# Order of the six products of a convolution set, and where their sums and ends are kept, in a two-layer Trainium2 kernel

## The chip, the cores and the metric

The kernel runs on one core of one Trainium2 chip, as one program. The metric is device time in microseconds (us) of one execution. Five engines work side by side and meet through semaphores: TensorE (PE in the profile; its weight loads are PEld), VectorE (DVE), ScalarE (ACT), GpSimd (POOL), and SyncE (SP), which here issues most DMAs. Each engine takes its own instructions strictly in the order in which the program lists them. PE writes only into PSUM, an accumulator memory of 8 banks of 512 float32 per partition; DVE and ACT read PSUM and carry results on to SBUF, the working memory.

## The reference, cut to what matters

Layer 0 (group norm, a four-direction state-space scan, a projection) and layer 1 act on x of shape 4 x 96 x 128 x 128. The change touches layer 1 alone. For each image x there is a split x1 = relu part, x2 = the rest, both normed, and then

```python
key   = unfold(conv2d(x1, aw1))          # 3x3, 96 -> 96 channels
qry   = unfold(conv2d(x2, aw2))
attn  = softmax(einsum('bckl,bqkl->bqck', key, qry).reshape(B, C, C*9) / sqrt(C*9))
value = conv2d(x1, aw3)
y1    = layer_norm(conv2d(value, attn.reshape(C, C, 3, 3)))   # weights made from the data
y2    = layer_norm(conv2d(x2, w_conv2)) * x1
out   = xr + conv2d(concat([y1, y2]), w_full) + b_full
```

So an image needs five 3x3 convolutions: aw1 and aw3 on x1, aw2 and w_conv2 on x2, and last the attention's own weights on value. All of it is float32.

## The kernel before, in words

**Stages.** From 0 to about 3685 us of the profiled execution come layer 0 for all four images and the convolutions of image 0, which are done directly, tap by tap (the group at L2156). From 3685 to about 6440 us comes the attention part of layer 1 (`attention`, L1946), and only there do the functions that the change touches run. After that the last image is written out.

**A convolution by products.** In the attention part a 3x3 convolution is done along the width with six products for every four neighbouring output columns: six planes of differences of the input (0 to 5, made earlier) are each multiplied with their own transformed weights on PE, which gives P0 to P5, and the outputs of the four columns are, with AA = 2,

- out 0 = P0 + (P1 + P2) + (P3 + P4)
- out 1 = (P1 - P2) + AA (P3 - P4)
- out 2 = (P1 + P2) + AA^2 (P3 + P4)
- out 3 = (P1 - P2) + AA^3 (P3 - P4) + P5

P1 to P4 are called the inner products here, P0 and P5 the outer ones (the code's `ends`). One call of `products` (L1443) is one set: 12 rows (`AR`) of an image, six products. Each product is two matmuls of 128 input rows (`main`, L1464, on the tiles `ya` and `yb`) and then small ones of 32 rows each (`rest`, L1479), because 3 taps x 96 channels are 288 = 128 + 128 + 32 rows. A float32 matmul is recorded as two matmuls in the profile.

**Which sets run.** Image 0 has 11 sets, one for each strip of 12 rows, with the attention's weights (`wa`; 96 output channels, 384 columns). Images 1 to 3 have those 11, and before them, in each strip, two maps of two sets: one of 128 output channels and 384 columns, whose output goes to `ring` and `own`, and one that puts two half strips side by side, 2 x 64 output channels and 192 columns, whose output goes to `own` or `oc` (weights `wd`). That is 44 + 132 = 176 sets. Between the sets of images 1 to 3, `taps.some` puts transposes of the ring (`both`, L1757) whose results ACT copies to `kt` (L1762), and the products of key and query (`multiplied`, L1632), which DVE adds to `sm` (L1645).

**PSUM tiles.** Sets, transposes and key-query products all take tiles called `two` from one pool (`pairs_of`, L1439): two banks each, three of them. A set takes three tiles: before, one for P0 and P5, which I call the outer tile; one for P1 and P3, the odd tile; one for P2 and P4, the even tile. PE may write into a tile only when every reader of the tile's last user is done. The other two banks of PSUM hold `bank` tiles of the work beside.

**A set before the change.** `products` does P0 and P5 first (the list `TWO`), and `outer` has ACT copy them to SBUF (`ends`, L1537), which frees the outer tile. Then come P1, P3, P2, P4 (`FOUR`). `sums` has ACT copy the odd tile to SBUF (`odd`, L1537), which frees it. Then DVE works on `odd` and the even tile: four operations on half tiles make P3 - P4 and P3 + P4 in SBUF (`wide`, L1551, L1552) and P1 - P2 and P1 + P2 in place in PSUM (L1553, L1554). Then it writes out 1 and out 2 (L1559), adds `ends` in place (L1557), and writes out 0 and out 3 (L1559). The even tile is free only after the last of these. Each of the four outputs takes one input from SBUF (`wide`) and one from PSUM.

**Who sets the order.** `later` is a list of postponed work that runs one step at each `tick()`. The program text gives each instruction a priority. From the attention part on, a scheduler of the tile framework places the instructions on their engines and picks a PSUM tile for each `two`, by priority and by its own model of when things are ready. The order on every engine is fixed by that before the run. Beside the sets runs other work (`light`): the norm of layer 0's output of the next image (L960, L1009), its split into x1 and x2 (L1250, L1254, and the difference planes on POOL and DVE: `pl`, `plv`, L1393 to L1429), and the output of the image before (L2271 to L2325). `co_run` (L298) interleaves the two by costs that the generators yield.

**Feeding.** `Attention.load` (L1885) brings the planes of a strip as three pairs of planes, by the list `PAIRS`; `turn` (L1913) has ACT copy parts of them to `yb` (L1925), six copies a strip, in the same order of pairs. `weights` (L1670) makes the attention's weights at the end of an image's maps: it runs a few steps of the last set before the softmax and a few behind it, to give PE work beside it.

Of the kernel before, what the change touches and what calls it, by code (L numbers as in the profile page):

```python
# [9 lines left out]
F32 = mybir.dt.float32  # L10
# [22 lines left out]
TN = W // TW  # L33
# [38 lines left out]
def kernel(  # L72
# [1272 lines left out]

    PAIRS = ((0, 5), (1, 3), (2, 4))
    PAIR = {i: k for k, pair in enumerate(PAIRS) for i in pair}
    SLOT = {i: pair.index(i) for pair in PAIRS for i in pair}  # L1350
    FOUR = ((1, 0), (3, 32), (2, 64), (4, 96))
# [87 lines left out]
    def pairs_of(ps):  # L1439

        return ps.tile([128, 2, CH], F32, name="two", tag="two")

    def products(ps, jobs, ws, later, evac, threes=False, fill=()):  # L1443


        w1, w2, w3 = ws
        share = sum(r * (e - p) for p, e, _, _, _, r in jobs) / (128.0 * AR)

        def tiles(v, o, r):
            v = v[:, o * TN : (o + r) * TN]  # L1450
            if threes:
                return v.rearrange("p (i q t) -> p q i t", q=3, t=TN)
            return v

        def of(to, r):
            to = to[:, : r * TN]
            if threes:
                return to.rearrange("p (q i t) -> p q i t", q=3, t=TN)
            return to

        def main(to, i):
            for k, w in enumerate((w1, w2)):
                for p, e, c, t, o, r in jobs:
                    nc.tensor.matmul(  # L1464
                        of(to[p:e], r),
                        lhsT=w[:, i, c : c + e - p],
                        rhs=tiles(t[k][PAIR[i]][:, SLOT[i]], o, r),
                        start=(k == 0),
                        stop=False,
                    )  # L1470

        def rest(j, group, to):
            for i, q in group:
                for p, e, c, (ya, _, (yc,)), o, r in jobs:
                    if q < 64:
                        rhs = tiles(yc[q : q + 32], o, r)
                    else:
                        rhs = tiles(ya[PAIR[i]][q : q + 32, SLOT[i]], o + (2 if q == 64 else 1), r)
                    nc.tensor.matmul(  # L1479
                        of(to[i][p:e], r),  # L1480
                        lhsT=w3[q : q + 32, j, c : c + e - p],
                        rhs=rhs,
                        start=False,
                        stop=True,
                    )

        outer, sums = evac
        fill = iter(fill)

        def beside():  # L1490
            for f in (next(fill, None),):
                if f:
                    f()

        a = pairs_of(ps)
        to = {0: a[:, 0], 5: a[:, 1]}
        for i, _ in TWO:
            main(to[i], i)
            beside()
            later.tick()  # L1500
            yield 1.3 * share
        rest(1, TWO, to)
        outer(a)
        later.tick()
        yield 0.4 + 0.4 * share
        a, b = pairs_of(ps), pairs_of(ps)
        to = {1: a[:, 0], 3: a[:, 1], 2: b[:, 0], 4: b[:, 1]}
        for i, _ in FOUR:
            main(to[i], i)
            beside()  # L1510
            later.tick()
            yield 1.3 * share
        rest(0, FOUR, to)
        sums(a, b)
        later.tick()
        yield 0.4 + 0.6 * share

    def outputs(pool, m, n, parts, later, then):

        got = []

        def at(v, k):
            if isinstance(v, list):
                return v[k]
            if len(v.shape) == 4:
                return v[:, :, k]
            return v.rearrange("p h (t k) -> p h t k", k=TW)[:, :, :, k]  # L1530

        def rows(v):
            return v.rearrange("p (h t) -> p h t", t=TN)

        def copy_of(x, name, bufs):
            t = pool.tile([128, 2, AR * TN], F32, name=name, bufs=bufs)[:m, :, :n]
            nc.scalar.copy(t, x[:m, :, :n])  # L1537
            return t

        def outer(c):  # L1540
            later(lambda: got.append(copy_of(c, "ends", 2)))

        def sums(a, b):
            def first():
                t = copy_of(a, "odd", 1)
                later(lambda: combined(t))

            def combined(t):
                w = pool.tile([128, 2, AR * TN], F32, name="wide", bufs=1)[:m, :, :n]
                ends, v = got[0], b[:m, :, :n]  # L1550
                nc.vector.tensor_sub(w[:, 1], t[:, 1], v[:, 1])  # L1551
                nc.vector.tensor_add(w[:, 0], t[:, 1], v[:, 1])  # L1552
                nc.vector.tensor_sub(v[:, 1], t[:, 0], v[:, 0])  # L1553
                nc.vector.tensor_add(v[:, 0], t[:, 0], v[:, 0])  # L1554
                for k, j, f in ((1, 1, AA), (2, 0, AA * AA), (0, 0, 1.0), (3, 1, AA**3)):
                    if k == 0:
                        nc.vector.tensor_add(v, ends, v)  # L1557
                    for p, e, o in parts:
                        nc.vector.scalar_tensor_tensor(  # L1559
                            at(o, k), rows(w[p:e, j]), f, rows(v[p:e, j]), ALU.mult, ALU.add  # L1560
                        )
                later(then)

            later(first)

        return outer, sums

    def by_threes(v, r):

# [9 lines left out]
    class Taps:  # L1579
# [4 lines left out]
        def __init__(self, ps, later, pool, slots, taps):  # L1584
            self.ps, self.later, self.pool, self.slots = ps, later, pool, slots
            self.taps = [(k, min(k + taps, KK)) for k in range(0, KK, taps)]
            self.sm = pool.tile([C, KK, C], F32, name="sm")
            self.rings = [pool.tile([128, 3, slots, PW], F32, name=f"ring{i}") for i in range(2)]
            for t in self.rings:
                nc.gpsimd.memset(t[:, :, :, 0:1].rearrange("p r i w -> p (r i) w"), 0.0)  # L1590
            self.groups, self.todo, self.rest = 0, [], ()

        def flat(self, m):
            return self.rings[m].rearrange("p r i w -> p (r i w)")
# [75 lines left out]
        def weights(self):  # L1670


            rest = iter(self.rest)
            self.later.flush()
            for _ in range(3):
                yield next(rest, 0.0)
            self.later.flush()
            while self.todo:
                yield from self.some(1)
                self.later.flush()  # L1680
            flat = self.sm.rearrange("p t o -> p (t o)")
            sc = 1.0 / math.sqrt(C * KK)
            mx = col("mx")
            nc.vector.reduce_max(mx, flat, AX.X)
            nc.vector.tensor_scalar(mx, mx, -sc, None, ALU.mult)
            den = col("den")
            nc.scalar.activation(flat, flat, AF.Exp, scale=sc, bias=mx, accum_out=den)
            nc.vector.reciprocal(den, den)
            nc.vector.tensor_scalar(flat, flat, den, None, ALU.mult)
            yield 4.0  # L1690
            for _ in range(2):
                yield next(rest, 0.0)

            v = self.flat(1)[0:C, : KK * C].rearrange("p (h w o) -> p h w o", h=3, w=3)
            for h in range(3):
                pT = self.part(C, 3 * C)
                for w in range(3):
                    nc.tensor.transpose(pT[:, w * C : (w + 1) * C], self.sm[:, 3 * h + w], ident)
                nc.vector.tensor_copy(v[:, h].rearrange("p w o -> p (w o)"), pT)
            wt = self.flat(0)[0:C, : 3 * NP * C].rearrange("p (h i o) -> p h i o", h=3, i=NP)  # L1700
            s = self.flat(1)[0:C, KK * C : 12 * C].rearrange("p (h o) -> p h o", h=3)
            products_weights(wt, v, s)
            self.wt = wt
            yield from rest
            self.later.flush()
            yield 4.0

    class PairTaps(Taps):
# [3 lines left out]
        def __init__(self, ps, later, pool):  # L1712
            self.ps, self.later, self.pool = ps, later, pool
            self.taps = [(0, 5), (5, KK)]
            sm = pool.tile([128, KK, C], F32, name="sm")
            self.sm = sm[0:C]
            self.spare = sm[96:128].rearrange("p t o -> p (t o)")
            self.rings = [
                pool.tile([128, 2, AR, JW], F32, name=f"ring{i}", tag=f"ring{i}") for i in range(2)
            ]  # L1720
            for t in self.rings:
                for j in range(TW):
                    nc.gpsimd.memset(t[:, :, :, JB * j + TN : min(JB * (j + 1), JW)], 0.0)
            self.todo, self.rest = [], ()

        def flat(self, m):
            return self.rings[m].rearrange("p s r w -> p (s r w)")
# [956 lines left out]
```

## Time and profile before

| what | value |
|---|---|
| median of 3 timed runs | 6458.6 us (6457.25 to 6462.66) |
| profiled execution, its own time | 6482.78 us |
| its span, first to last instruction | 6481.0 us |
| granted TensorE clock, mean | 0.887 |
| stretch 0 to 3685 us: busy PE, DVE, ACT, POOL | 2988, 2727, 2322, 2302 us |
| stretch 3685 to 6440 us (attention part) | shown below in the prediction |
| stretch 6440 to 6481 us: busy PE, DVE | 30.6, 19.5 us |

How to read the lines below. A row of groups has the line in the program, the engine, the operation, out<-in by the program's names, a shape and a count; behind the first bar the busy time in us and the mean of one in ns; behind the second bar the engine's idle time just before them and what ended most of it. A row of waits names an engine and the line that waited, what it waited for, the total in us, how often, and the longest. A row of the timeline has the start in us, the length in us, the engine, the line and, in square brackets, the idle time before it and what ended it. A row that begins with a stretch has its length and then, for each engine, busy us and the number of instructions, and last the granted clock, the share of DMA time, and GB/s.

### The profile page before, as it was taken

To read this page: it belongs to the slowest core of one execution; us is meant where nothing else is said; L and a number is where in the kernel's file an instruction comes from. 1 tells how busy PE (TensorE), PEld (TensorE's weight loads), DVE (VectorE), ACT (ScalarE), POOL (GpSimd) and SP (SyncE) were. 2 spreads that over 40 slices of the span, in tenths; PEclk is the share of its full clock that TensorE was granted. 3 is DMA by queue.
4 is the path that set the end of the run, shared out by engine and by line. 5 is a ranking of instruction groups with operands and counts; after the bars stand their busy time and mean duration, and the time that the engine had idled before them with its cause. 6 is when DMAs were issued, how large, how long until landed. Compare 5 with 4: busy or idle time off the path is not lost. (4 is left out here: it accounts for less than half of the span.)

```text
span 6481.0 us, 76143 instructions
## 1 busy us (share of the span) xinstructions
PE 5325.5 (82%) x23264; PEld 2306.2 (36%) x23264; DVE 4757.0 (73%) x7132; ACT 3792.2 (59%) x4770; POOL 3279.9 (51%) x2514
## 2 busy tenths in 40 slices
PE   6889988987887754989988588877888877889888
PEld 2333323322222111444433234345333445345543
DVE  4247878988999768988844785468874687988766
ACT  1247767777787676777632565366634665545542
POOL 1226757978889455969822344346313265023310
PEclk9899989988998666999998798888988888999989
DMA  6767777776775766675676775655776656966668
GB/s 154 175 156 193 197 206 191 216 211 165 205 196 157 214 179 213 196 208 176 192 189 182 189 217 158 165 157 153 215 195 171 174 141 165 245 173 179 184 168 217
DMA packets 884520, 1205.17 MB, mean 186 GB/s; under 512 B 220084, under 2 KB 736570, under 8 KB 871632
## 3 DMA queue, kind: packets, MB, share of 16 engines
q1 hardware_dynamic: 860496, 1145.35, 65.1%
q0 software_dynamic: 16208, 38.42, 2.3%
q10 hardware_dynamic: 7408, 16.53, 0.8%
q8 instruction: 187, 3.06, 0.2%
q14 instruction: 221, 1.81, 0.1%
HBM read 777.82 MB, written 345.62 MB: 173 GB/s over the span
## 5 line engine op out<-in xcount | busy, mean ns | idle before, releaser
L629 PE MATMUL bank<-y,wp 128*128 128x512 f32 (+3 forms) x3584 | 1315.6, 624 | 85.4 <-DMA y<-y 42.2
L862 POOL TENSOR_TENSOR y<-y,dl 128x1024 f32<-128x1024 f32 x384 | 1055.6, 2749 | 262.5 <-DVE dl L854 236.5
L829 POOL TENSOR_TENSOR dl<-dl,u 128x1024 f32<-128x1024 f32 x384 | 1008.2, 2626 | 264.7 <-ACT dA L805 123.5
L850 DVE TENSOR_TENSOR_SCAN dA<-dA,pBC 128x512 f32<-128x512 f32 x768 | 981.6, 1278 | 30.7
L1464 PE MATMUL two<-ya,wd 128*64 128x192 f32 (+3 forms) x2376 | 588.8, 422 | 197.8 <-ACT odd L1537 80.0
L629 PEld LDWEIGHTS bank<-y,wp 128*128 128x128 f32 (+3 forms) x3584 | 458.6, 169 | 755.4 <-issue 654.4
L743 PE MATMUL pBC<-xr,wbc 60*128 60x512 bf16 (+1 forms) x1536 | 460.7, 406 | 316.5 <-DVE dA L850 245.8
L2156 PE MATMUL bank<-y,wn 128*64 128x384 f32 (+5 forms) x2408 | 674.9, 505 | 54.7 <-DMA y<-x1d 31.6
L854 DVE TENSOR_TENSOR dl<-dA,pBC 128x512 f32<-128x512 f32 x768 | 528.3, 688 | 260.7 <-PE pBC L743 187.2
L1925 ACT COPY yb<-ya 64x768 f32<-64x768 f32 (+1 forms) x660 | 537.5, 814 | 196.1 <-PE two L1464 130.2
L672 ACT ACTIVATE dl<-pd,dtb 128x512 f32<-128x512 f32 x768 | 486.4, 684 | 190.0 <-PE pd L743 172.3
L1464 PE MATMUL two<-yb,wd 128*64 128x192 f32 (+3 forms) x2376 | 563.5, 407 | 4.0 <-ACT yb L1925 4.0
L833 DVE TENSOR_TENSOR pBC<-dl,pBC 128x512 f32<-128x512 f32 x768 | 527.5, 687 | 8.5 <-POOL dl L829 7.5
L2156 PEld LDWEIGHTS bank<-y,wn 128*64 128x64 f32 (+3 forms) x2408 | 309.8, 168 | 347.0 <-issue 164.1
L805 ACT ACTIVATE dA<-dl,negA 128x1024 f32<-128x1024 f32 x384 | 420.3, 1142 | 2.3
L1464 PEld LDWEIGHTS two<-ya,wd 128*64 128x64 f32 (+1 forms) x2376 | 265.9, 169 | 398.5 <-ACT odd L1537 90.6
L743 PEld LDWEIGHTS <-wbc 60*128 60x128 bf16 (+1 forms) x1536 | 103.7, 96 | 764.3 <-issue 750.7
L672 ACT ACT_TABLE_LOAD x248 | 318.2, 1283 | 93.8 <-PE pd L743 80.7
L1464 PEld LDWEIGHTS two<-yb,wd 128*64 128x64 f32 (+1 forms) x2376 | 293.7, 171 | 147.3 <-issue 34.1
L2265 POOL MEMSET o<- 1x1024 f32 x60 | 56.4, 947 | 540.6 <-PE bank L2320 220.4
L1009 PE MATMUL bank<-y,outws 96*96 96x512 f32 x512 | 312.1, 748 | 13.2 <-DVE r L1022 7.7
L1464 PE MATMUL two<-ya,wa 128*96 128x384 f32 (+1 forms) x528 | 231.1, 521 | 71.8 <-DMA wa<-watd 27.0
(316 smaller groups left out, 9370.8 us busy)
## 6 DMA issues: line engine op xcount, KB each, us to landing
u<-zb SPq DMA_DIRECT2D x192, 1024.0 KB
yms<-y SPq DMA_DIRECT2D x96, 512.0 KB
y<-yms SPq DMA_DIRECT2D x64, 768.0 KB
xn<-xnew SPq DMA_DIRECT2D x128, 384.0 KB
ya<-vp SPq DMA_DIRECT2D x120, 336.0 KB
y<-y SPq DMA_DIRECT2D x128, 258.2 KB
zb<-z SPq DMA_DIRECT2D x64, 512.0 KB
ya<-x1p SPq DMA_DIRECT2D x90, 336.0 KB
```

The lines of the kernel that those rows point to most:

```text
L629: nc.tensor.matmul(blocks(pz[p:e]), lhsT=ws[k][:, d, c : c + e - p], rhs=window(ys[k], at, d, n), start=(i == 0), stop=(i == len(terms) - 1),)
L672: nc.scalar.activation(dst, src, AF.Softplus, bias=bias)
L743: nc.tensor.matmul(p, lhsT=w[rows], rhs=xr[rows, at : at + CH], start=True, stop=True)
L805: nc.scalar.activation(live[m]["dA"], live[m]["dl"], AF.Exp, scale=negA[:, g % 3, k : k + 1])
L829: nc.gpsimd.tensor_mul(t, t, u_view(n))
L833: nc.vector.tensor_mul(p, live[n]["dl"][:, bass.ts(half, CH)], p)
L850: nc.vector.tensor_tensor_scan(h, h, p, init, ALU.mult, ALU.add)
L854: nc.vector.tensor_mul(live[n]["dl"][:, sl], live[n]["dA"][:, sl], live[n]["C", half])
L862: nc.gpsimd.tensor_add(v, v, t.rearrange("p (a b) -> p a b", b=W))
L1464: nc.tensor.matmul(of(to[p:e], r), lhsT=w[:, i, c : c + e - p], rhs=tiles(t[k][PAIR[i]][:, SLOT[i]], o, r), start=(k == 0), stop=False,)
L1925: nc.scalar.copy(yb[k][64 * h - 64 : 64 * h, :, :n], ya[k][0:64, :, h * TN : h * TN + n])
L2156: nc.tensor.matmul(pc[p:e, :n].rearrange("p (h w) -> p h w", w=W), lhsT=w[:, c : c + e - p], rhs=v[:, :, 0:W], start=(i == 0), stop=(i == ...
```

## The change

The inner products go first and the outer ones last. The list of pairs is turned in the same way, so planes 1 and 3 are loaded and copied first, then 2 and 4, then 0 and 5. ACT still copies the odd tile to SBUF. DVE then makes all sums and differences in two operations on whole tiles instead of four on half tiles, into one SBUF tile `sums` (128 x 2 x 2 x 384, one buffer; `wide`, 128 x 2 x 384, one buffer, and `ends`, 128 x 2 x 384, two buffers, go). Out 1 and out 2 are written from `sums` alone, both inputs in SBUF. The outer tile isn't copied by ACT any more: once P0 and P5 are there, DVE adds the first half of `sums` to it in place in PSUM, and writes out 3 and out 0 from it and `sums`. The even tile is free after the two operations; the outer tile is free after out 0. In `weights` the number of steps of the last set ahead of the softmax is 2 and behind it 3 for images 1 to 3 (before: 3 and 2), and stays 3 and 2 for image 0.

```diff
-    PAIRS = ((0, 5), (1, 3), (2, 4))
+    PAIRS = ((1, 3), (2, 4), (0, 5))
...
     def products(ps, jobs, ws, later, evac, threes=False, fill=()):
...
-        outer, sums = evac
+        sums, ends = evac
...
+        a = pairs_of(ps)
+        to = {1: a[:, 0], 3: a[:, 1]}
+        for i, _ in FOUR:
+            if i == 2:
+                b = pairs_of(ps)
+                to |= {2: b[:, 0], 4: b[:, 1]}
+            main(to[i], i)
+            beside()
+            later.tick()
+            yield 1.3 * share
+        rest(0, FOUR, to)
+        sums(a, b)
+        later.tick()
+        yield 0.4 + 0.6 * share
         a = pairs_of(ps)
         to = {0: a[:, 0], 5: a[:, 1]}
         for i, _ in TWO:
...
         rest(1, TWO, to)
-        outer(a)
+        ends(a)
         later.tick()
         yield 0.4 + 0.4 * share
-        a, b = pairs_of(ps), pairs_of(ps)
-        to = {1: a[:, 0], 3: a[:, 1], 2: b[:, 0], 4: b[:, 1]}
-        for i, _ in FOUR:
-            main(to[i], i)
...
-        rest(0, FOUR, to)
-        sums(a, b)
-        later.tick()
-        yield 0.4 + 0.6 * share
...
     def outputs(pool, m, n, parts, later, then):
-        got = []
+        made = []
...
-        def outer(c):
-            later(lambda: got.append(copy_of(c, "ends", 2)))
+        def out(k, x, f, y):
+            for p, e, o in parts:
+                nc.vector.scalar_tensor_tensor(
+                    at(o, k), rows(x[p:e]), f, rows(y[p:e]), ALU.mult, ALU.add
+                )
...
             def combined(t):
-                w = pool.tile([128, 2, AR * TN], F32, name="wide", bufs=1)[:m, :, :n]
-                ends, v = got[0], b[:m, :, :n]
-                nc.vector.tensor_sub(w[:, 1], t[:, 1], v[:, 1])
-                nc.vector.tensor_add(w[:, 0], t[:, 1], v[:, 1])
-                nc.vector.tensor_sub(v[:, 1], t[:, 0], v[:, 0])
-                nc.vector.tensor_add(v[:, 0], t[:, 0], v[:, 0])
-                for k, j, f in ((1, 1, AA), (2, 0, AA * AA), (0, 0, 1.0), (3, 1, AA**3)):
-                    if k == 0:
-                        nc.vector.tensor_add(v, ends, v)
-                    for p, e, o in parts:
-                        nc.vector.scalar_tensor_tensor(
-                            at(o, k), rows(w[p:e, j]), f, rows(v[p:e, j]), ALU.mult, ALU.add
-                        )
-                later(then)
+                u = pool.tile([128, 2, 2, AR * TN], F32, name="sums", bufs=1)[:m, :, :, :n]
+                v = b[:m, :, :n]
+                nc.vector.tensor_sub(u[:, :, 1], t, v)
+                nc.vector.tensor_add(u[:, :, 0], t, v)
+                out(1, u[:, 1, 1], AA, u[:, 0, 1])
+                out(2, u[:, 1, 0], AA * AA, u[:, 0, 0])
+                made.append(u)
+
+            later(first)
+
+        def ends(c):
+            def closed():
+                if not made:
+                    later(closed)
+                    return
+                u, v = made[0], c[:m, :, :n]
+                nc.vector.tensor_add(v, u[:, 0], v)
+                out(3, u[:, 1, 1], AA**3, v[:, 1])
+                out(0, u[:, 1, 0], 1.0, v[:, 0])
+                later(then)
...
     class Taps:
+            self.held = (3, 2)
...
     class PairTaps(Taps):
+            self.held = (2, 3)
```

## The prediction

> **What bounds the kernel now.** The change acts only in the attention part, so I read that stretch alone. The chain of waits at the end is no guide: it reaches back to 6421 us only. First the engines over the stretch:
>
> ```profile
> 3685.00:6440.00 2755.00, 2306.70 (x12304) 1199.11 (x12305) 2010.92 (x3490) 1470.59 (x1945) 972.57 (x1352) 0.89 0.68 181
> ```
>
> PE is busy 2307 of 2755 us (84%), DVE 73%, ACT 53%, POOL 35%. PE is the backbone and loses some 450 us. Next, what PE waited for in the stretch:
>
> ```profile
> PE two L1464 <- ACT odd L1537: 95.4, 37, 10.0
> PE two L1464 <- ACT kt L1762: 51.4, 30, 7.9
> PE two L1464 <- ACT ends L1537: 37.5, 18, 6.5
> ...
> PE two L1464 <- ACT yb L1925: 21.8, 15, 3.6
> ...
> PE two L1464 <- DVE sm L1645: 19.2, 19, 3.4
> PE two L1632 <- ACT odd L1537: 16.7, 16, 3.3
> ...
> PE two L1632 <- DVE ring L1559: 13.7, 10, 4.4
> ...
> PE two L1464 <- DVE ring L1559: 9.5, 9, 2.7
> PE two L1757 <- ACT odd L1537: 9.1, 7, 2.6
> ```
>
> A matmul does not read `odd`, `ends` or `kt`: PE waits there for a PSUM tile that the copy frees. Odd makes 95.4 + 16.7 + 9.1 = 121 us, ends 37.5, kt some 59 with its L1632 rows, sm some 21, and DVE's L1559 (end of the even tile, or of the ring) some 28: 267 us in all. The timeline shows the plainest case:
>
> ```profile
> 4593.19 0.80 ACT L1537 COPY odd<-two 96x768 f32<-96x768 f32 x1
> ...
> 4594.03 0.89 PE L1464 MATMUL two<-ya,wa 128*96 128x384 f32 x2 [2.25 <-ACT odd L1537]
> ...
> 4594.76 0.81 PE L1464 MATMUL two<-yb,wa 128*96 128x384 f32 x2
> ```
>
> The odd copy starts late (ACT was busy with the split), and the next set's first product starts as it ends. Products follow each other at about 0.65 us for 384 columns. In the built program that set's outer tile takes the place of the odd tile just finished, though three tiles exist. Last, what the change removes or alters:
>
> ```profile
> L1557 DVE TENSOR_TENSOR two<-ends,two 128x384 f32<-128x384 f32 (+5 forms) x176 | 138.9, 789 | 3.9
> L1559 DVE SCALAR_TENSOR_TENSOR own<-wide,two 96x384 f32<-96x384 f32 (+3 forms) x296 | 133.4, 493 | 8.7 <-DMA od<-own 5.3
> ...
> L1537 ACT COPY ends<-two 128x384 f32<-128x384 f32 (+5 forms) x176 | 116.0, 659 | 242.3 <-PE two L1479 219.4 <-DVE two L1557 22.2
> ...
> L1553 DVE TENSOR_TENSOR two<-odd,two 128x192 f32<-128x192 f32 (+5 forms) x176 | 83.2, 473 | 3.7
> ...
> L1551 DVE TENSOR_TENSOR wide<-odd,two 128x192 f32<-128x192 f32 (+5 forms) x176 | 81.2, 461 | 189.3 <-ACT odd L1537 155.8 <-PE two L1479 32.5
> ```
>
> **The change, part by part.** PE's matmuls, weight loads and the DMAs are the same in number and size; the built programs agree (ACT loses 176 instructions, DVE 352). Only their order differs, from the attention part on.
>
> *ACT.* 176 copies of `ends` go: 116.0 us busy. ACT is idle for half of the stretch, so on its own this is worth little. It shortens the queue ahead of odd, kt and yb copies; of the 21.8 us that PE waits for yb I take 3 as saved.
>
> *DVE, sums.* L1551 to L1554 cost 81.2 + 80.9 + 83.2 + 83.2 = 328.5 us. Two whole-tile operations replace them. The nearest row has the same shape and one PSUM input (L1557, 789 ns): 352 x 0.789 = 278 us, so 51 us less.
>
> *DVE, outputs.* Out 3 and out 0 keep one PSUM input. Out 1 and out 2 now have both in SBUF; they are half of L1559's 311 us, 156 us. Undisturbed, such an operation costs the same: a 96x288 one with SBUF inputs (L1295) has a median of 448 ns, the 128x288 form of L1559 averages 449. But POOL disturbs it: the split's SBUF differences (L1393, 96x256 on DVE) have a minimum of 399, a median of 415 and a maximum of 2786 ns, and in this stretch a mean of 635, while the PSUM form of L1254 stays at 711 to 791. The tax is bounded by the `e` operations (L2277, 96x1024 in SBUF: mean 1324 over a median of 1274 ns, +4%) and by L1393's mean (+53%): +6 to +82 us. The new outputs run at all times, not just beside plane-making, so I take +20%, 31 us. DVE then ends 20 us lower, between 45 lower and 31 higher; off the bound, I count it as 0.
>
> [...]
>
> *PSUM tiles, where the gain must come from.* For each of the 742 uses of a `two` tile in both built programs I took the PE work that lies between the last write of its former user and the first write of the new one, at 0.65 us for a full 384-column product. A reuse with under 2.5 us of it is tight: a copy of 0.66 us and a little queue eat it up. Before, tight reuses number 127 behind an odd tile, 62 behind an outer tile, 97 behind kt, 34 behind sm. That prices one at 121/127 = 0.96, 37.5/62 = 0.60, 59/97 = 0.61 and 21/34 = 0.62 us. After:
>
> - odd: 77 x 0.96 = 74 us (was 121). Where it is left, the outer tile often takes the odd tile's place within the set, so a wait of one copy stays there.
> - kt: 86 x 0.61 = 52 (was 59); sm: 14 x 0.62 = 9 (was 21).
> - outer: freed by DVE's add and two outputs, 0.79 + 2 x 0.49 = 1.77 us, instead of a copy; so I count reuses under 3.6 us: 35 x 0.60 = 21 (was 37.5).
> - even: freed after the copy and two operations, 0.66 + 2 x 0.79 = 2.24 us, where before DVE's whole work of 5 us lay ahead. But it is reused much sooner: 90 have under 4.1 us, so 90 x 0.60 = 54 (was 28).
>
> Sum 210 instead of 267: 57 us less. The bounds: if even and outer reuses wait no more than they did (28) or not at all (0), it is 163 and 104 us less; if each costs the odd tile's 0.96, it is 255 and 12 us less. I take the middle, because ends-like waits are the nearest to a release by a short operation.
>
> *Waits added.* DVE's in-place add now waits for P0 and P5. Queued behind it on DVE are out 3, out 0 and the work beside (split, norm, output); PE waits for that work only in the rows L1022, L2312 and the like. Before, DVE stood 189 us ahead of L1551 for the odd copy, so it has such a place already; I count 0, and the price without cover is the slower rival's. The turned pairs move no transfer past another in number or size: 0. Of the last set's eight steps five are held in both, 3 + 2 before, 2 + 3 after: 0.
>
> *End.* After the last matmul DVE does L1551 to L1554 and two outputs ahead of the add (6429.76 to 6432.24); these 2.5 us leave the end.
>
> Sum: 57 + 3 + 2.5 = 62 us of 6482.8, the profiled execution's time (span 6481.0), so 6421. The median of the timed runs is 24 us lower; by the same difference I forecast **6397 us**, with 6350 (104 + 5 less) to 6445 (12 less) for this case alone.
>
> **Rivals.** *Slower: DVE becomes the gate of PSUM.* DVE now frees two of a set's three tiles, not one, and its queue holds operations like L1393's longest of 2.8 us, while its own outputs get longer under POOL. If each of the 176 outer reuses costs an odd reuse's 0.96 us (169 us) instead of 21, and the even ones 54 as above, the 62 gained turn into 86 lost: 6545 at worst, and with half of the outer reuses hit 6471, the point from which it decides. I centre it at 6490. For it: DVE at 73%, over 85% in some stretches. Against: only 5 outer reuses have under 2.5 us.
>
> *No change: the wait moves on.* PE stops a little later, at yb copies, at loads (DMA share 0.68, above 0.9 in places) or at the output's DVE work, which a denser order of sets pushes together: in the built program the output of image 0 stands in one run of 48 products without a set, before the longest was 20. At DVE's 7 us for each four of them PE would idle some 40 us there, against some 24 now. Then 6446 to 6471.
>
> *Much faster:* waits of 7 to 10 us shrink too, and PE's clock, 0.89 here, rises with fewer gaps: 6330.
>
> **How the numbers follow.** Forecast's case 0.60, much faster 0.08, no change 0.11, slower 0.21. About 0.2% (13 us) is what a measurement can tell from no change: faster means under 6446 and holds the first two, 0.68; same 0.11; slower 0.21. The range starts at 6350, which leaves out most of the 0.08, and must take in no change and the near half of the slower case: 6485.
>
> **What would show it.** Right: PE's waits for odd fall to some 75 us, those for ends vanish, new ones for DVE's add and outputs stay under 80; ACT's busy time falls by 116, DVE's by about 20; out 1 and out 2 average under 0.6 us. Wrong: DVE's in-place add or outputs lead PE's waits with over 150 us, or PE's idle time in the attention part stays near 450.

## The result and the profile after

The changed kernel takes 6465.75 us (median of 14 runs), the kernel before 6462.3 us on the same chip (14 runs): a ratio of 1.0006, 95% interval 0.9994 to 1.0017. On a second chip it was 1.0008 (0.9995 to 1.0021). That is no change, where 62 us less were forecast. The profiled execution after took 6465.84 us, with a span of 6463.7 us; that it lies 17 us under the profiled execution before goes with the granted clock, 0.891 against 0.887: PE's idle time is the same.

First the attention part of the changed kernel in one stretch (length; then PE, weight loads, DVE, ACT and POOL with busy us and instructions; clock, DMA share, GB/s):

```profile
3685.00:6440.00 2755.00, 2300.74 (x12336) 1196.34 (x12337) 2002.16 (x3146) 1366.33 (x1769) 986.28 (x1355) 0.90 0.69 182
```

ACT has lost its copies, DVE a little, and PE gained nothing. Added up over the trace, from the wait ahead of the first product of a set on, PE's idle time was 474 us before (471 in a second profile) and is 478 now (473 and 476 in two more). Where it stands has changed, though. PE's waits in the attention part after:

```profile
PE two L1464 <- ACT kt L1770: 55.4, 34, 7.1
PE two L1464 <- DVE own L1540: 43.4, 20, 5.4
PE two L1464 <- ACT odd L1547: 36.7, 30, 6.1
PE bank L2329 <- DVE c L2320: 29.9, 24, 3.1
PE two L1765 <- ACT odd L1547: 27.9, 7, 7.5
PE two L1464 <- issue: 27.0, 12, 5.7
...
PE two L1464 <- DVE ring L1540: 17.1, 11, 7.5
PE two L1464 <- DVE sm L1653: 16.9, 6, 5.7
PE two L1464 <- ACT yb L1933: 16.4, 8, 5.9
...
PE two L1464 <- DVE sums L1554: 14.1, 9, 4.8
...
PE two L1765 <- DVE sums L1554: 11.4, 7, 3.9
PE two L1640 <- ACT odd L1547: 10.8, 5, 4.1
...
PE two L1640 <- ACT kt L1770: 6.0, 5, 1.9
...
PE two L1640 <- DVE ring L1540: 5.0, 2, 4.1
```

The waits for `odd` have fallen from 121 to 36.7 + 27.9 + 10.8 = 75 us and those for `ends` are gone. In their place stand waits that DVE ends: L1540 (out 3 and out 0, which free the outer tile) and L1554 (the second whole-tile operation, which frees the even tile). The "issue" row belongs to them as well. Each of its twelve waits ends 0.1 us after a DVE instruction that frees a tile, eight after L1554 (20.3 us) and four after L1540 (6.6 us); "issue" only means that the profile ties no semaphore event to the wait. With these, the outer tile makes 73 us and the even tile 46.

The groups of the new operations, in the same stretch:

```profile
L1567 DVE TENSOR_TENSOR two<-sums,two 128x384 f32<-128x384 f32 (+5 forms) x176 | 138.5, 787 | 45.7 <-PE two L1479 43.4
L1553 DVE TENSOR_TENSOR sums<-odd,two 128x384 f32<-128x384 f32 (+5 forms) x176 | 136.9, 778 | 191.1 <-ACT odd L1547 174.4 <-PE two L1479 16.2
L1554 DVE TENSOR_TENSOR sums<-odd,two 128x384 f32<-128x384 f32 (+5 forms) x176 | 136.5, 776 | 0.0
...
L1540 DVE SCALAR_TENSOR_TENSOR ring<-sums 128x384 f32<-128x384 f32 (+1 forms) x132 | 87.2, 698 | 0.0
...
L1540 DVE SCALAR_TENSOR_TENSOR ring<-sums,two 128x384 f32<-128x384 f32 (+1 forms) x132 | 66.3, 538 | 1.2
```

The durations are those of the prediction: 137 us for each whole-tile operation, and the outputs with two SBUF inputs dearer than those with one, 698 ns against 538 for the same shape.

The clearest single case, PE's and then DVE's timeline of the changed kernel (start, length, instruction, idle time before it):

```profile
3750.52 0.89 PE L1479 MATMUL two<-ya,wa 32*96 32x384 f32 x4
...
3763.69 0.89 PE L1479 MATMUL two<-ya,wa 32*96 32x384 f32 x4
3769.76 1.59 PE L1464 MATMUL two<-ya,wa 128*96 128x384 f32 x2 [5.19 <-DVE own L1540]
```

```profile
3753.93 0.93 DVE L1553 TENSOR_TENSOR sums<-odd,two 96x768 f32<-96x768 f32 x1
3754.79 0.94 DVE L1554 TENSOR_TENSOR sums<-odd,two 96x768 f32<-96x768 f32 x1
3755.83 0.96 DVE L1567 TENSOR_TENSOR two<-sums,two 96x768 f32<-96x768 f32 x1
3756.70 1.40 DVE L1254 SCALAR_TENSOR_TENSOR half<-xn,kept,bank 96x512 f32<-96x512 f32 x2
...
3764.68 1.40 DVE L1254 SCALAR_TENSOR_TENSOR half<-xn,kept,bank 96x512 f32<-96x512 f32 x2
3766.00 2.32 DVE L1540 SCALAR_TENSOR_TENSOR own<-sums 96x384 f32<-96x384 f32 x2
3768.16 1.55 DVE L1540 SCALAR_TENSOR_TENSOR own<-sums,two 96x384 f32<-96x384 f32 x2
```

A set's outer tile gets its last product at 3751.4 (3750.52 + 0.89). DVE adds to it at 3755.8, turns to 9.3 us of other work (L1254 and, left out above, the split's differences), makes out 1 and out 2, and is done with out 3 and out 0 at 3769.7. PE has had nothing to do since 3764.6, and starts again 0.05 us after the release. The tile was held for 18.3 us after its last product.

That is one of the longer cases. Over all 176 sets of this profile the outer tile was held, from its last product to its release, for 8.6 us on average, with a median of 6.3 us, and 120 times for over 3.6 us. In the kernel before, where ACT copied it away, the mean was 1.8 us and the median 0.85 us.

### The profile page after: what moved, and what is told of

It is laid out like the page before. It is cut to its first block, busy times and chain, and to the rows that moved or that the text cites. A ratio compares the mean times of both kernels' runs of the same rounds, so it can differ in the third digit from the quotient of the medians.

```text
span 6463.7 us, 75769 instructions
## 1 busy us (share of the span) xinstructions
PE 5304.1 (82%) x23264; PEld 2295.9 (36%) x23264; DVE 4739.6 (73%) x6780; ACT 3688.3 (57%) x4594; POOL 3290.3 (51%) x2514
## 3 DMA queue, kind: packets, MB, share of 16 engines
q14 instruction: 216, 1.77, 0.1%
## 5 line engine op out<-in xcount | busy, mean ns | idle before, releaser
L1547 ACT COPY odd<-two 128x384 f32<-128x384 f32 (+5 forms) x176 | 116.2, 660 | 419.3 <-PE two L1479 298.4
```

## The experiments

Twelve runs were made: eight new kernels, one of them twice, the kernel before once more, and the changed kernel twice more. The ratios hold a kernel against the kernel before on its own chip; the second profiles of the kernel before and of the changed one are single executions without a ratio. The table has PE's waits by the tile that was freed, in us, from one profile each ("issue" waits put to the DVE instruction that they follow by 0.1 us), and PE's idle time from the wait ahead of the first product of a set on. The long wait ahead of that first product (26 to 27 us) is in none of the columns by tile.

| kernel | ratio to before (95%) | odd | outer | even | kt | yb | PE idle |
|---|---|---|---|---|---|---|---|
| before, two profiles | 1 | 123, 121 | 38, 37 | 34, 38 | 59, 60 | 22, 21 | 474, 471 |
| changed, three profiles | 1.0006, 1.0008 | 75, 78, 76 | 73, 74, 78 | 46, 42, 45 | 61, 55, 58 | 16, 18, 18 | 478, 473, 476 |
| add into SBUF | 1.0079 (1.0059–1.0099) | 83 | 98 | 61 | 29 | 26 | 485 |
| outer tile copied | 0.9959 (0.9945–0.9974) | 68 | 57 | 50 | 24 | 50 | 446 |
| the same again | 0.9940 (0.9919–0.9960) | 61 | 46 | 57 | 25 | 51 | 447 |
| outer outputs first | 1.0020 (1.0010–1.0030) | 75 | 68 | 55 | 47 | 20 | 462 |
| spare copy of the outer tile | 1.0100 (1.0085–1.0116) | 73 | 102 | 50 | 65 | 11 | 506 |
| order alone | 1.0057 (1.0044–1.0070) | 90 | 117 | 49 | 29 | 18 | 496 |
| spare copy of `odd` | 1.0069 (1.0050–1.0088) | 75 | 100 | 50 | 48 | 23 | 498 |
| all three copied | 1.0111 (1.0091–1.0130) | 68 | 59 | 64 | 26 | 65 | 509 |
| copy freed by the add | 0.9973 (0.9960–0.9987) | 76 | 44 | 57 | 17 | 53 | 452 |

**The two kernels again.** No edit.

> The kernel before once more, for a second profile of it. It shows how far the sums of PE's waits differ between two executions of one program. Every theory expects the same: in the attention part PE waits for a PSUM tile freed by the odd copy about 120 us, by the ends copy about 38, by kt about 59, by the outputs 34, by sm 21, each within some 15 us.

> The changed kernel once more, for a second profile. In the first one PE waited about 75 us for the odd copy, 72 for the outer tile (freed by DVE's last two outputs, some of it shown as issue), 46 for the even tile (freed by DVE's second whole-tile sum), 61 for kt, 19 for sm. Theory A (the outer tile's release stands in DVE's queue behind the split's differences): outer again 55 to 90 us over 30 to 45 waits, near 2 us each. If the first profile was a chance, outer is below 40.

> The changed kernel on the chip of this call, so that the others are held against it here. All theories: 0.999 to 1.002 of the kernel before; outer waits 65 to 80 us, odd 70 to 80, kt 55 to 62, even 40 to 48.

The waits by tile repeat within some 6 us in these two kernels (within 11 us in the kernel with the copied outer tile, below), though the times of single executions lie up to 40 us apart. So the waits can be read from one profile, and the outer tile's 73 us are no chance: 37 to 40 waits of 1.8 to 2.0 us on average. The third run, on another chip, gave 1.0008.

**The add into SBUF.**

```diff
-                nc.vector.tensor_add(v, u[:, 0], v)
-                out(3, u[:, 1, 1], AA**3, v[:, 1])
-                out(0, u[:, 1, 0], 1.0, v[:, 0])
+                nc.vector.tensor_add(u[:, 0], u[:, 0], v)
+                out(3, u[:, 1, 1], AA**3, u[:, 0, 1])
+                out(0, u[:, 1, 0], 1.0, u[:, 0, 0])
```

> One edit on the changed kernel: the last add writes its sum into SBUF, over u[:, 0], and out 3 and out 0 read SBUF only. The outer tile is then free after DVE's add and not after the two outputs, which stand 5 to 10 us behind it where the split's differences come between. Theory A: the waits for the outer tile fall from 72 to some 35 us, DVE's outputs 3 and 0 cost 20 to 35% more (155 us become 185 to 210), and the time falls by 20 to 40 us against the changed kernel (6425 to 6445). Rival B (PE's idle time is fixed by what feeds it, ACT's copies of the inputs and the loads, and the slot waits only show it): the outer waits fall as much, others grow by as much, time within 10 us. Rival C (DVE's busy time is what counts): slower by 20 to 50 us, since DVE gets more work.

Theory A failed here: some 35 us of outer waits were expected, and they rose to 98. The release did come earlier, at a median of 4.3 us after the tile's last product where the changed kernel has 6.3. But it is still DVE's, and the built program has tighter places: 69 reuses behind outer have under 3.6 us of PE work between, where the changed kernel has 35. Rival C gave the right sign, but the next kernel has about the same DVE work (2023 us busy in the stretch, 2020 here, 2002 in the changed kernel) and is the fastest.

**The outer tile copied by ACT.**

```diff
+            def copied():
+                t = pool.tile([128, 2, AR * TN], F32, name="ends", bufs=1)[:m, :, :n]
+                nc.scalar.copy(t, c[:m, :, :n])
+                got.append(t)
+                later(closed)
...
-                u, v = made[0], c[:m, :, :n]
+                u, v = made[0], got[0]
...
-            later(closed)
+            later(copied)
```

> On the changed kernel, ACT copies the outer tile to SBUF as it did before, and DVE adds and makes out 3 and out 0 from SBUF. The order of the set, the two whole-tile sums and outputs 1 and 2 stay as changed. The outer tile is freed by ACT. Theory A: outer waits fall from 72 to 20 to 40 us; ACT's busy time grows by 116 us, which puts odd at 75 to 100; time 20 to 45 us under the changed kernel. Rival B: within 10 us of the changed kernel. Rival D (ACT's queue is the scarce one, and the copy removed was the gain): odd and kt waits rise by 40 us or more together, time 10 to 30 us above the changed kernel.

> The kernel with the copied outer tile once more, on the chip of this call, to hold its ratio of 0.9959 [0.9945, 0.9974] against a second measurement, and its waits (ends 57, odd 68, even 49, yb 49, kt 24 us) against a second profile. If it is a gain and not a chance of one chip: 0.993 to 0.998, each of the waits within 12 us.

Two chips agree: 0.41% and 0.60% under the kernel before, 28 and 39 us, and about 30 us of PE's idle time less than in the changed kernel. Theory A's time came (20 to 45 us under the changed kernel were expected, by the ratios it is some 30); its number for the outer waits did not (20 to 40 us expected, 57 and 46 measured). The tile is free at a median of 1.6 us after its last product.

The nearest kernel to hold it against is "add into SBUF". Both have their last add and all outputs in SBUF, and DVE is busy about as long. They differ in who takes the outer tile out of PSUM: DVE there, an ACT copy here. They are not otherwise alike, though. From the first product of a set on, PE's matmuls stand in another order at 2901 of 12367 places of the two traces (at none between two profiles of one kernel), and the built program has more tight reuses behind outer here, 116 under 3.6 us of PE work against 69. The waits of the two, add into SBUF first:

```profile
PE two L1464 <- DVE sums L1567: 97.1, 49, 9.1
PE two L1765 <- ACT odd L1547: 33.8, 9, 8.3
...
PE two L1464 <- issue: 27.0, 13, 5.5
PE two L1464 <- ACT yb L1933: 25.8, 10, 8.8
```

```profile
PE two L1464 <- ACT ends L1574: 57.1, 35, 6.3
PE two L1464 <- ACT yb L1939: 49.5, 27, 9.9
...
PE two L1771 <- ACT odd L1547: 33.6, 7, 12.8
PE two L1646 <- ACT odd L1547: 30.7, 12, 6.6
PE two L1464 <- DVE sums L1554: 25.1, 13, 9.3
```

The outer tile goes from 98 to 57 us although more of its reuses are tight, `odd` and even fall by 15 and 11, `yb` takes 24 back, PE's idle time falls by 39 us, and the median time by 77 (6492.1 to 6415.0). ACT has 116 us more work in the faster one. The built program names the tile of every matmul, so each wait can be laid on its reuse. Reuses with over 5 us of PE work between make 50 of the 98 us in "add into SBUF" and 52 of the 73 in the changed kernel, but 1 of the 57 here. Where DVE frees the tile, PE still waits for it after that much other work; where ACT copies it, hardly ever. Part of the 77 is not in this comparison of profiles: the profiled execution of "add into SBUF" (6469 us) was the quickest of its six.

**The outer outputs first.** Outputs 1 and 2 are issued behind outputs 3 and 0.

```diff
-                out(1, u[:, 1, 1], AA, u[:, 0, 1])
-                out(2, u[:, 1, 0], AA * AA, u[:, 0, 0])
                 made.append(u)
...
                 out(0, u[:, 1, 0], 1.0, v[:, 0])
+                out(1, u[:, 1, 1], AA, u[:, 0, 1])
+                out(2, u[:, 1, 0], AA * AA, u[:, 0, 0])
```

> One edit on the changed kernel: outputs 1 and 2 are issued behind outputs 3 and 0. In two profiles of the changed kernel PE waited 73 and 74 us for the outer tile, and in these waits DVE was at the outputs themselves for some 51 us. Theory A (the outer tile's release stands behind DVE's own outputs): with two of the four moved behind the release, the outer waits fall from 73 to 40 to 55 us and the time by 15 to 35 us against the changed kernel, that is to 0.998 to 1.001 of the kernel before. Theory A2 (what stands ahead is other DVE work, the split's above all): the outer waits stay within 10 us, time too. Rival B (PE's idle time is fixed elsewhere): waits fall, others grow, time within 10 us of the changed kernel.

The narrow form of theory A fails, and it goes as A2 had it: the outer waits make 68 us against 73 to 78, now in 44 waits and not 40, the even tile waits 55 us for 46, and by the ratios the time is some 8 us above the changed kernel. The outer tile is held as long as before the edit (a median of 6.0 us from its last product, 6.3 in the changed kernel). So it isn't the two outputs ahead that make the release late. PE's idle time is some 14 us less than in the changed kernel all the same; why the time doesn't follow it is not shown.

**A spare copy of the outer tile on ACT.** Nothing reads it, and DVE still frees the tile.

```diff
+            def spare():
+                t = pool.tile([128, 2, AR * TN], F32, name="spare", bufs=1)[:m, :, :n]
+                nc.scalar.copy(t, c[:m, :, :n])
+
+            later(spare)
             later(closed)
```

> On the changed kernel, ACT copies the outer tile into a spare tile that nothing reads; DVE's in-place add and outputs stay as they are, so the tile is still freed by DVE. This adds 176 copies of 0.66 us, 116 us, to ACT. It asks what ACT's 116 us are worth. The prediction's step (ACT is idle for half of the stretch, 3 us): time within 15 us of the changed kernel, odd waits 75 to 95 us. Rival D (ACT's queue is scarce): odd, kt and yb waits rise by 40 us or more and the time by as much. In either case outer waits stay at 60 us or more if theory A holds, since the copy does not free the tile.

This one answers another question than the one asked. DVE's in-place add overwrites what the copy reads, so it had to wait for it (70 us of DVE's idle time ahead of the add were ended by the copy), and the outer waits grew to 102 us. Odd and yb did not grow. So a release put behind one more step cost PE time here (506 us of idle time, 473 to 478 in the changed kernel); whether ACT's load does, the next kernel asks without a new wait.

**A spare copy of `odd`.**

```diff
                 later(lambda: combined(t))
+                x = pool.tile([128, 2, AR * TN], F32, name="spare", bufs=1)[:m, :, :n]
+                nc.scalar.copy(x, t)
```

> On the changed kernel, ACT copies the finished odd copy, in SBUF, once more into a spare tile that nothing reads: 176 copies, some 116 us, without a new wait between engines and with the changed kernel's places of the PSUM tiles (77 tight reuses behind odd, 39 behind outer under 3.6 us of PE work, against 77 and 35). The prediction's step (ACT's 116 us are worth 3 us): time within 15 us of the changed kernel, odd 75 to 85 us, kt 55 to 65, yb 15 to 25. Rival D (ACT's queue is scarce, and taking the copy away was a gain of tens of us that something else took back): odd, kt and yb together rise by 40 us or more, and the time by 30 us or more.

The time rose by 37 us against the changed kernel on the same chip (medians of 6485.3 and 6448.0 us), so the prediction's "3 us" for ACT's 116 is too low. Rival D's time came (30 us or more), but not by its waits: odd, kt and yb make 146 us, against 152 in the changed kernel. The outer waits rose from 78 to 100 us:

```profile
PE two L1464 <- DVE own L1540: 48.8, 21, 6.0
...
PE two L1464 <- DVE ring L1540: 39.6, 20, 11.3
```

So a busier ACT shows at the tile that DVE frees. By which chain is not shown. DVE's split work waits for ACT (L1254 reads what L1250 wrote; 26.3 us of DVE's idle time ended so), which would make the release later, but on average the outer tile is held no longer (8.7 us from its last product, 8.6 in the changed kernel). Of all the edits this one moves the rest least: PE's matmuls stand in another order at 104 of 12367 places.

**The order alone.** The inner products first, with the arithmetic of the kernel before: ACT copies the outer tile, four half-tile operations and the add write into the even tile in PSUM.

```diff
             def combined(t):
...
-                nc.vector.tensor_sub(u[:, :, 1], t, v)
-                nc.vector.tensor_add(u[:, :, 0], t, v)
+                nc.vector.tensor_sub(w[:, 1], t[:, 1], v[:, 1])
+                nc.vector.tensor_add(w[:, 0], t[:, 1], v[:, 1])
+                nc.vector.tensor_sub(v[:, 1], t[:, 0], v[:, 0])
+                nc.vector.tensor_add(v[:, 0], t[:, 0], v[:, 0])
```

> The new order of the set with the arithmetic of the kernel before: inner products first, ACT copies the outer tile, four half-tile sums and the add into the even tile, outputs from the even tile in PSUM. In its built program reuses under 2.5 us of PE work number 135 behind odd, 82 behind outer, 97 behind kt, 26 behind sm, against 127, 62, 97 and 34 before. Theory A (time follows the tight reuses and the price of who frees the tile): odd 110 to 135 us, ends 45 to 60, kt about 60, time 0 to 25 us above the kernel before. If the order of the products were itself the gain that showed with the copied outer tile (0.9959), this kernel would be near 0.996 too.

It is 0.57% slower than before, a little beyond theory A's range, with 117 us of waits for the copied outer tile where 45 to 60 were expected, and 90 for `odd` where 110 to 135 were. In the built program the tight reuses of tiles that the `ends` copy reads number some 138 and those of `odd` 90, so the expectation seems to have the two exchanged. The order by itself loses. The even tile is now held until the outer products have come and all outputs are made, 14.3 us on average from its last product (12.6 in the kernel before), and in the kernel with the copied outer tile 6.9. So it is the second part of the change, the two operations that free the even tile, with which the order pays.

**All three copied.** ACT copies the even tile as well, into `sums`, on top of the copied outer tile.

```diff
+                v = u[:, :, 0]
+                nc.scalar.copy(v, b[:m, :, :n])
...
-                nc.vector.tensor_add(u[:, :, 0], t, v)
+                nc.vector.tensor_add(v, t, v)
```

> On the kernel with the copied outer tile, ACT copies the even tile too, so that ACT frees all three tiles of a set, and DVE works in SBUF alone. ACT gets 116 us more; DVE's two whole-tile sums have two SBUF inputs and may grow by 10 to 30%. Theory A (a tile freed behind DVE's queue costs more than one freed by an ACT copy): the 49 us of waits for the even tile fall to 15 to 35 us, time 0 to 25 us under the kernel with the copied outer tile, that is 0.992 to 0.996 of the kernel before. Rival D: ACT, at 232 us above the changed kernel, is late for odd, ends and yb; their waits rise by more than the even tile's fall, time 0.998 or more. Rival C (DVE's time decides): slower than the kernel with the copied outer tile by the 30 to 80 us that the sums grow.

1.1% slower, so "ACT frees" is no rule by itself. The copy fills the one buffer of `sums`, which the set before still reads, and now ACT stands in line for DVE:

```profile
L1550 ACT COPY sums<-two 128x384 f32<-128x384 f32 (+5 forms) x175 | 116.0, 663 | 130.6 <-DVE own L1540 60.4 <-DVE ring L1540 43.2 <-PE two L1479 13.5
```

Of the 130.6 us that ACT idled ahead of these copies, DVE's outputs ended 103.6. The two sums went from 777 to 930 and 887 ns, now that both inputs lie in SBUF, which is 43 us more of DVE's time (rival C). What the waiting copies and the longer sums cost apart is not shown.

**The copy freed by the add.** On the kernel with the copied outer tile, the add writes over `u[:, 0]`, as in the first experiment, so that the one buffer of `ends` is free two outputs earlier.

```diff
-                nc.vector.tensor_add(v, u[:, 0], v)
+                nc.vector.tensor_add(u[:, 0], u[:, 0], v)
```

> On the kernel with the copied outer tile, DVE's add writes its sum over u[:, 0] and no longer into the copy, so that the one copy buffer is free after the add. In that kernel ACT stood 57 us ahead of the copy for DVE's outputs of the set before, which still read the buffer. Theory A (the copies on ACT free the PSUM tiles; what delays a copy delays the tile): ACT's waits for DVE ahead of the copy fall from 57 to under 20 us, PE's waits for ends, odd and yb (57, 68 and 49 us) fall together by 20 to 50 us, time 10 to 30 us under the kernel with the copied outer tile. Against it: in its built program 67 reuses behind outer are tight, against 40; at the 1.4 us that one cost there, 57/40, this takes back 38 us. So theory A with the places of the tiles counted in: within 20 us of the kernel with the copied outer tile. If neither places nor ACT's wait matter: the same time.

ACT's wait ahead of the copy stayed at 50 us (it had been 57), now ended by the add. The ends, odd and yb waits make 44 + 76 + 53 = 173 us, against 174 and 158 in the two profiles of the kernel with the copied outer tile, so no fall shows. The time is 21 us above that kernel on the same chip (6427.9 against 6407.1), more than PE's idle time explains (452 us against 447). The granted clock was lower too, 0.885 to 0.891 against 0.890 to 0.894. The kernel with the copied outer tile stays the best of the study: the change without its last part, with the last add and out 3 and out 0 working on the copy.

## Why the prediction was wrong

**The sum.** 57 of the 62 us were to come from 210 us of waits for PSUM tiles instead of 267. By the prediction's own rows they are 75 + 61 + 19 + 73 + 46 = 274. Its terms, with the first profile after: odd 74, measured 75; kt 52, measured 61; sm 9, measured 19; even 54, measured 46; **outer 21, measured 73**.

**The failed step** is that term, "35 x 0.60 = 21". It holds that the outer tile is free 1.77 us after its last product, so that only the 35 reuses with under 3.6 us of PE work can wait, at the price of a tight reuse behind an ACT copy. I had counted the service time of the add and two outputs and left out the time in DVE's queue. The release came at a median of 6.3 us, not 1.77. So the waits fall elsewhere than counted: of the 73 us, 5 lie on reuses with under 3.6 us of PE work, and 52 on reuses with over 5 us, which the prediction took as free. In the kernel before, 30 of the 37.5 us lay on reuses under 2.5 us and 5 on those over 5 us, so the method fitted a tile that ACT frees. That PE waited 37 to 40 times, near the 35 counted, is chance, since they are not the same reuses. Nor did a single wait get longer: 1.8 us on average before, in 21 waits, and 1.8 to 2.0 after. The 0.60 us was a price per tight reuse, most of which made no wait.

The rows I had were enough to doubt the step: L1559, the release by DVE's outputs before, stood at 28 us although no reuse behind the even tile had under 2.5 us of PE work. Of the prediction's signs, PE's idle time in the stretch staying near 450 us meant wrong, and it is 454 (2755.00 - 2300.74). The limit of 80 us for new waits on DVE's add and outputs was kept (73 us), but it stood so far above the 21 us of the sum that it could not tell right from wrong. One reading of the waits was loose as well, without weight in the sum: the products of key and query (L1632) do read `kt`, so the 7.7 us of their rows need not be waits for a tile.

**The rivals.** The time is that of "no change" (0.11), but not for its reasons: yb waits fell from 22 to 16 us, and those for the output's DVE work stayed at 33 (21.8 + 11.5 before, 29.9 + 3.5 after), though the run of 48 products is there. What happened is the mechanism of the slower rival, DVE as the gate of PSUM, at under half of its worst price: 52 of the 57 us go back at the outer tile. My argument against it, "only 5 outer reuses have under 2.5 us", used a threshold that fits a tile freed by a copy of 0.66 us.

**What held.** DVE's sums: 278 us forecast, 136.9 + 136.5 = 273 measured. The outputs from SBUF alone: 87.2 + 73.5 + 27.8 + 2.9 = 191 us, 23% over the half of 311 (20% was taken). The waits for odd came within 1 us of the forecast, those for `ends` are gone, and out 1 and out 2 average 0.54 us (under 0.6 was the sign). ACT's busy time in the stretch fell by 104 us (116 forecast), DVE's by 9 (20 forecast). After the last product DVE needs 1.6 us to the last output, before 4.1, the 2.5 us of the end.

**What ACT's copy was worth.** I counted 3 us, from ACT's idle half. The spare copy of `odd` shows that 121 us more on ACT cost 37 us here. It doesn't show that taking 116 away wins as much.

**The three parts together**, each as a kernel: the order alone +0.57%; with the two operations into SBUF and the outer tile still copied, −0.41% and −0.60%; with the copy left out, +0.06% and +0.08%. By these kernels the change earned its gain with its second part and gave it back with its third, which looked like pure saving.

**What stays open.** What stands in line ahead of the release is known in sum only. Of the time in which the outer tile was held after its last product in the changed kernel, DVE spent 40% on the sets' own sums and outputs, 57% on the work beside (the output of the image before and the split above all), and was idle for 4%. Which of it could stand elsewhere was not tried. The built program also places the tiles anew with every edit, and PE's order moves too, so that no experiment changes one thing only. That the late release behind DVE makes the outer tile's 73 us is measured; how much of the 28 to 39 us of the best kernel comes from the copy itself, and how much from the new places, stays open.

## What to carry to other kernels

Price the release of a scarce buffer by the queue of the engine that frees it, not by the length of the instruction: a 0.66 us copy on a half-idle engine can be cheaper than no copy and a release behind a busy one (here by some 30 us). A count of tight reuses needs the real time of release, queue included, or it leaves out the waits that matter (here 52 of 73 us). Before an operation is removed because its engine has time, ask what it let go early. And where a change has several parts, build it without each of them; here the best kernel was the change less its last part.

## What the runs showed of the hardware

The time of one and the same program goes with the granted clock: the six executions of "add into SBUF" ran at clocks of 0.890, 0.888, 0.888, 0.887, 0.886 and 0.884, and took 6469, 6491, 6493, 6489, 6502 and 6513 us. That spread is most of what was to be measured, so the comparison of two single profiled times (6482.8 before, 6465.8 after) says nothing; PE's idle time, from the same profiles, repeats within 5 us.

That the clock is higher where PE has fewer gaps, as the much faster rival has it, shows within the profile of the kernel before: of the 27 stretches of 100 us from 3700 to 6400, the seven with PE busy for under 80 us had a clock of 0.75 to 0.88, the six with over 90 us one of 0.84 to 0.98. From kernel to kernel no rise shows: on one chip the profile of the kernel before, with 471 us of PE's idle time, has 0.893, that of the kernel with the copied outer tile, with 446 us, 0.891.

The tax on operations with two SBUF inputs is not one number: 538 to 698 ns (30%) for 128x384 outputs, 493 to 539 (9%) for the largest `own` group, 501 to 504 for the last outputs, those to `o`, where POOL is nearly idle (busy 8.25 of the 140 us from 6300 on). It goes with POOL. Of the 120 outputs of 128x384 that the changed kernel makes from SBUF alone, the 73 with no POOL instruction beside them took 549 ns on average, the 47 with one 974 ns; the same outputs with one PSUM input took 549 and 545.
